# A two-layer graph network on one core: the opening stage reordered, the first group's weight factors read where they were made, x1 in four tiles

## The chip, the cores and the metric

The kernel runs on one core of a Trainium2 chip. The metric is the device time of that core in microseconds (us), from the start of the program to its end. All data are 32-bit floats.

The core has five engines that each run their own list of instructions in order. TensorE (PE) multiplies matrices; loading its stationary operand is shown apart as PEld. VectorE (DVE), ScalarE (ACT) and GpSimd (POOL) work element by element. SyncE (SP) issues transfers here. Engines wait for each other through semaphores, and an instruction that waits holds up all that stands behind it on its engine. Transfers between the large memory and the on-chip memory are served by 16 DMA engines.

## The reference

There are 128 batches of 128 nodes with 512 features, and one adjacency matrix `adj` of 128 x 128. Layer 0 normalizes each node, takes the positive part, mixes the nodes by `adj` and multiplies by a 512 x 512 weight; layer 1 is masked attention with 8 heads of 64, a projection, and a second normalization:

```python
h = jnp.maximum(_layernorm(x, axis=-1), 0.0)
x = x + (jnp.einsum('nm,bmd->bnd', adj, h) @ L0_weight + L0_bias)
h = jnp.maximum(_layernorm(x, axis=-1), 0.0)
q, k, v = heads of (h @ w_qkv)
attn = softmax(where(adj == 0, -inf, q @ k.T * scale))
o = (attn @ v) @ w_proj + b_proj
x = x + o + layernorm(o) * gamma + beta
```

## The kernel before

**Stages.** A batch passes through these steps; the names are those of tiles and functions in the code. `load` brings x. `norm0` takes statistics of x on VectorE, an inverse root `rs` on GpSimd and `shift` on VectorE; ScalarE makes h0 from them (L262), and GpSimd adds the bias of layer 0 to x (L265). `mix` multiplies h0 by the turned adjacency matrix on TensorE (L274) and ScalarE copies the result to yT. Layer 0's product with w0 follows, and VectorE adds x to it, which gives x1. `norm1` makes h1 in the same way (L318); h1 is written to the large memory and read back in four pieces (`exchange`, L208 and L213), so that VectorE's 32 x 32 transposes can finish the turn of the matrix (`flip`, L334). `keep_x1` adds beta to x1 on GpSimd (L325) and stores it as x1d, to be read again at the end. Then come q, k and v, the scores, the softmax, attention, projection and the output (`finish`, `finish_out`, `finish_last`).

**Seven products instead of eight.** Large products run as 2 x 2 blocks with seven block products (the Strassen-Winograd scheme). This needs sums of blocks on both sides. On the activation side GpSimd makes four sums (`left_factors`, L222; the tiles are hsum, ysum and osum). On the weight side four differences are made once (`combine_qkv`, `combine_one`, L149, on VectorE). For q, k and v a group of four batches is multiplied at once: three kinds (the three calls of `qkv` with kind 0, 1 and 2), seven products each (L362), from one weight block for each product. The weight blocks don't all fit on the chip. So the three plain blocks are fetched from the weight itself, and the four differences are first written to the large memory (`SUMS`, tile wt, L150) and fetched from there, into one of five tiles wq (`fetch`, L156). The differences are made in tiles that later stages use for other things: sx, pT, s, e, o, oT, x1b and t.

**The opening.** The first eight batches (`AHEAD`) run before anything else is there to overlap with. Their layer 0 is one plain product of eight matmuls for each batch (`layer0_whole`, L458, result pd), without the scheme. Its two result banks d0 and d1 alternate between batches, so the product of a batch waits until VectorE has added the result of the batch two before (L648). x1 has three tiles: the sum of batch 5 takes the tile of batch 2, and so waits for batch 2's store x1d.

**Order.** The code has no loop over stages. Each step is put into a list with a due time (`put`), the list is worked off by due time, and that fixes the order of instructions on each engine. The due times do not delay anything on the chip: they only set the order. `mix_at`, `h0_at`, `START` and `when` give the due times that the change touches. All transfers but a few at the start stand in one list, that of SyncE.

**Banks of the seven products.** Products 0 and 2 (counted from 0), then 4 and 6, collect in one bank, 1 and 3 in another, 5 in a third. A result is read out between two products of its bank, by ScalarE (`start`, L366) after products 0, 1, 2 and 6, and by VectorE (`add`, L251) after 3, 4 and 5. So product 4 waits until ScalarE has copied the result of product 2.

Of the kernel before, what the change touches and what calls it, by code (L numbers as in the profile page):

```python
# [9 lines left out]
F32 = mybir.dt.float32  # L10
AF = mybir.ActivationFunctionType
ALU = mybir.AluOpType
AX = mybir.AxisListType

P = 128
# [5 lines left out]
def kernel(  # L21
# [30 lines left out]
    nc = tc.nc  # L52
    B, N, D = x.shape
# [3 lines left out]
    G = 4  # L57
    Q, R = 4, 32
    F = D // 2
# [4 lines left out]
    work = ctx.enter_context(tc.tile_pool(name="work", bufs=2))  # L64
    stat = ctx.enter_context(tc.tile_pool(name="stat", bufs=8))
    dram = ctx.enter_context(tc.tile_pool(name="dram", bufs=3, space=bass.MemoryType.DRAM))
    psum = ctx.enter_context(tc.tile_pool(name="psum", bufs=1, space=bass.MemoryType.PSUM))
# [3 lines left out]
    X, H0, YT, X1, X1D, H1, H1T, WQ, QKT, V, S, PT, OT, O, X1B, LEFT0, LEFT1, LEFT2 = ({} for _ in range(18))  # L71

    def load(i):
        X[i] = work.tile([P, D], F32, name="x", bufs=6)
        nc.sync.dma_start(out=X[i], in_=x[i])
# [7 lines left out]
    w0_sb = const.tile([P, 7, 2, F], F32)  # L83
    wp_sb = const.tile([P, 7, 2, F], F32)
    b0_b = const.tile([P, D], F32)
    bp_b = const.tile([P, D], F32)
    gamma_b = const.tile([P, D], F32)
    beta_b = const.tile([P, D], F32)

    def block(w, row, col):  # L90

        return w[row * F:(row + 1) * F, col:col + F].rearrange("(c p) o -> p c o", p=P)

    BLOCKS = (0, 4), (5, 3)

    def load_square(eng, w_sb, w):

        for row, places in enumerate(BLOCKS):
            for col, k in enumerate(places):
                eng.dma_start(out=w_sb[:, k], in_=block(w, row, col * F))  # L100

    def broadcast(eng, t, src):
        eng.dma_start(out=t, in_=src.partition_broadcast(P))
# [9 lines left out]

        combine(eng, w[:, 0], w[:, 4], w[:, 5], w[:, 3], w[:, 1], w[:, 2], w[:, 4], w[:, 6])

    load_square(nc.scalar, w0_sb, w0)
    for i in range(2, 4):
        load(i)
    broadcast(nc.scalar, b0_b, b0)

# [2 lines left out]
    def qkv_block(kind, row, col):  # L125
        return block(w_qkv, row, 2 * D + col * F if kind == 2 else col * D + kind * F)
# [3 lines left out]
    def load_qkv(kind, *names):  # L130

        pieces = []
        for name, bufs, shape in names:
            t = work.tile(shape, F32, name=name, bufs=bufs)
            t = t if len(shape) == 2 else t.rearrange("p a b -> p (a b)") if len(shape) == 3 else \
                t.rearrange("p a b c -> p (a b c)")
            pieces += [t[:, n:n + D].rearrange("p (c o) -> p c o", c=2) for n in range(0, t.shape[1], D)]
        for n in range(4):
            nc.sync.dma_start(out=pieces[n], in_=qkv_block(kind, n // 2, n % 2))
        return pieces  # L140

    def combine_qkv(eng, t, kind, pieces):
# [15 lines left out]
    ident = const.tile([P, P], F32)  # L158
# [4 lines left out]
    maskb = const.tile([P, P], F32)  # L163

    def turn_adj():
        pa = psum.tile([P, P], F32, tag="at", name="pa", bufs=4)
        nc.tensor.transpose(pa, adj_sb, ident)
        nc.scalar.copy(adjT, pa)

    def make_mask():  # L170


        edge = const.tile([P, P], F32)
        some = const.tile([P, 1], F32)
        nc.vector.tensor_scalar(edge, adj_sb, 0.0, None, op0=ALU.not_equal)
        nc.vector.tensor_reduce(some, edge, AX.X, ALU.max)
        nc.vector.reciprocal(some, some)
        nc.vector.tensor_scalar(some, some, 0.0, None, op0=ALU.mult)
        nc.vector.tensor_scalar(edge, edge, 1.0, MASKED, op0=ALU.subtract, op1=ALU.mult)
        nc.vector.tensor_scalar(maskb, edge, some, None, op0=ALU.add)  # L180
# [22 lines left out]
    def exchange(t, dst, src):  # L203


        w = src.shape[2]
        d = dram.tile([P, Q, w], F32, name=f"d{w}")
        nc.sync.dma_start(out=d, in_=src)  # L208
        put(t, exchange_back, dst, d)
# [87 lines left out]

    def layer0_whole(i, t):
        p = whole(YT, i, lambda row, col: w0_sb[:, BLOCKS[row][col]])
        X1[i] = work.tile([P, D], F32, name="x1", bufs=3)  # L300
        put(t + 3.6, nc.vector.tensor_tensor, X1[i], p, X.pop(i), ALU.add)

    def layer0(j):
        for b in (2 * j, 2 * j + 1):
            X1[b] = work.tile([P, D], F32, name="x1", bufs=3)
        return pair_chain(LEFT0.pop(j), w0_sb, (X1[2 * j], X1[2 * j + 1]), (X.pop(2 * j), X.pop(2 * j + 1)),
                          "d0", "d1")

# [7 lines left out]
    def norm1_out(i, t, arg):  # L316
        h1 = work.tile([P, Q, C, R], F32, name="h1")
        nc.scalar.activation(h1.rearrange("p q c r -> p c q r"), X1[i].rearrange("p (c q r) -> p c q r", c=C, q=Q),  # L318
                             AF.Relu, **arg)
        H1[i] = work.tile([P, Q, C * R], F32, name="h1x")  # L320
        exchange(t + 4.5, H1[i], h1.rearrange("p q c r -> p q (c r)"))
        put(t + 1.5, keep_x1, i)

    def keep_x1(i):
        nc.gpsimd.tensor_tensor(X1[i], X1[i], beta_b, op=ALU.add)  # L325
        X1D[i] = dram.tile([P, D], F32, name="x1d", bufs=20)
        nc.sync.dma_start(out=X1D[i], in_=X1.pop(i))

# [153 lines left out]
        put(t + 3, finish_last, i, n, X1B.pop(i))  # L482

    def finish_last(i, n, x1):
        nc.gpsimd.tensor_tensor(n, n, x1, op=ALU.add)
        nc.sync.dma_start(out=out[i], in_=n)

# [8 lines left out]
    BEGIN, LAST, AHEAD = -3, B - G, 8  # L496
    START = BEGIN * SHORT - 38.5
    later, count = [], [0]

    def put(t, f, *a):  # L500
        count[0] += 1
        heapq.heappush(later, (t, count[0], f, a))

    def when(i, us):
        return i * SLOT + us if i >= 0 else i * SHORT + us * SHORT / SLOT

    def mix_at(i):
        return START + i * STEP if i < AHEAD else when(i - 10, (11.6, 9.2)[i % 2])

    def h0_at(i):  # L510
        return mix_at(i) - 1.2 if i < AHEAD else when(i - 11 - i % 2, 13.2 if i % 2 else 12)

    def run(make, times):

# [18 lines left out]
    t, last = when(LATE, 0), ""  # L533
# [8 lines left out]
    def scores_at(i):  # L542
        return when(i - i % 2, 2 + i % 2) if i < LATE else AT["s"][i - LATE]
# [20 lines left out]
    GROUP = (3.9, 6.5, 9.05, 13.3, 16.75), (1.5, 4.1, 6.7, 11.0, 14.4)  # L564
    for i in range(B):
        if i >= 4:
            put(START - 3 + i if i < 6 else mix_at(i - 6) + 10 if i < AHEAD + 6 else when(i - 13, 0), load, i)
        put(mix_at(i), mix, i, mix_at(i))
        put(scores_at(i), scores, i, scores_at(i))
        put(flip_at(i), flip_probs, i)  # L570
        put(attend_at(i), attend, i, attend_at(i))

    for j in range(B // 2):
        a, b = 2 * j, 2 * j + 1
        i = a - 8
        if a < AHEAD:
            t = mix_at(a) - 5
            put(t, norm0, j, t)
            for n in (a, b):
                t = mix_at(n) + 5.2  # L580
                put(t, layer0_whole, n, t)
            t += 4.4
            flips = t + 11.7, t + 12.7
        else:
            t = when(i - 3, 5.2)
            put(t, norm0, j, t)
            t = when(i - 1, 12)
            put(t, pair_left, j, t, 2.5, YT, LEFT0, "ysum")
            run(lambda j=j: layer0(j), [when(i, p) for p in PAIR[0]])
            t = when(i, PAIR[0][6]) + 1.5  # L590
            flips = when(i + 2, 7.5), when(i + 2, 9)
        put(t, norm1, j, t)
        put(flips[0], flip, a)
        put(flips[1], flip, b)

        i = a + 5
        t = attend_at(b) + 2
        if b < LAST:
            put(t, pair_left, j, t, 3.4 if i < LATE else 1.5, OT, LEFT2, "osum")
            n = 7 * (a - LATE + 4) // 2  # L600
            times = [when(i, p) for p in PAIR[1]] if i < LATE else AT["p"][n:n + 7]
            run(lambda j=j: project(j), times)
            ends = [((a, b), when(i + 1, 1.2) if i < LATE else times[6] + 2.2)]
        else:
            ends = []
            for n in (a, b):
                t = AT["D"][n - LAST]
                put(t, project_whole, n, t)
                ends.append(((n,), t + 4.6))
        for batches, t in ends:  # L610
            for n in batches:
                put(t - 7 + 3 * (n % 2), reload, n)
            put(t, finish, batches, t)

    steps = []
    for g in range(B // G):
        i = g * G - 3
        t, gap = (START + 36.2, 1.4) if g == 0 else (when(i - 1, 13), 4) if i < LATE else (TAIL + 9.8, 2.2)
        put(t, group_left, g, t, gap)
        times = sorted(when(i + n, p) for n in range(G) for p in GROUP[(i + n) % 2] + ((13.1,) if n == 0 else ()))  # L620
        if i + G > LATE:
            n = sum(t < TAIL for t in times)
# [2 lines left out]
            run(lambda g=g, kind=kind: qkv(g, kind), times[7 * kind:7 * kind + 7])  # L625
        steps += [(t, g, n // 7, n % 7) for n, t in enumerate(times)]
    for n, (t, *a) in enumerate(steps):
        put(steps[n - 4][0] + 0.1 if n >= 4 else t - 10, fetch, *a)

    put(START - 6, turn_adj)  # L630
    put(when(-2, 2), make_mask)
# [4 lines left out]
        put(t - 12, lambda kind=kind, t=t, tiles=tiles: combine_qkv(nc.vector, t, kind, load_qkv(kind, *tiles)))  # L636
    put(when(-2, 9), combine_square, nc.gpsimd, w0_sb)
    put(START + 8, broadcast, nc.sync, beta_b, beta)
    put(when(0, 12), load_square, nc.sync, wp_sb, w_proj)
    put(when(1, 3), broadcast, nc.sync, bp_b, b_proj)  # L640
    put(when(1, 4), broadcast, nc.sync, gamma_b, gamma)
    put(when(2, 12), combine_square, nc.gpsimd, wp_sb)
# [3 lines left out]
    while later:  # L646
        t, _, f, a = heapq.heappop(later)
# [30 lines left out]
```

## Time and profile before

| what | before |
|---|---|
| time, median of three runs | 2381.83 us (2381.12 to 2382.42) |
| span of the profiled run | 2388.1 us |
| TensorE busy, with 14105 matmuls | 2335.9 us, 98% |
| VectorE, ScalarE, GpSimd busy | 67%, 44%, 70% |
| idle time of TensorE from 0 to 90 us | 18.9 us |
| idle time of TensorE from 2250 us to the end | 21.9 us |
| start of the first qkv product | 52.61 us |
| start of the second kind's, of the third kind's first product | 76.6 us, 90.45 us |

The profile has groups of instructions, each with a line of the code, an engine, and its operands as `out<-in`. The idle time of an engine stands in brackets, with what ended it: `DMA wq<-wt` means that the data had not landed. TensorE runs at one of two clock rates, and PEclk or the clock column is the share of the full rate that was granted. 32-bit matmuls show as two records each, so eight records are four matmuls. A record's length holds a tail in which the next has begun; the difference between two starts is the better price.

### The profile page before, as it was taken

The numbers are of one execution on the slowest core, as the hardware profiler recorded it, in microseconds if no ns is written. First come the engines' busy times: TensorE is split into PE (matmuls) and PEld (weight loads), VectorE is DVE, ScalarE is ACT, GpSimd is POOL, SyncE is SP. The second block draws the span as 40 slices with busy tenths as digits, with TensorE's granted clock in tenths as the row PEclk, the third lists the DMA queues.
The fourth block names the chain that finished last, engine by engine and source line by source line (L and its number), as shares of the span: only waits on it lengthen the run. The fifth ranks groups of instructions, "written<-read, shape, count | busy, mean of one in ns | idle before, by whom it ended". The sixth has DMA issues, their size and how long they took to land.

```text
span 2388.1 us, 42653 instructions
## 1 busy us (share of the span) xinstructions
PE 2335.9 (98%) x14105; PEld 2052.5 (86%) x14105; DVE 1604.7 (67%) x3225; ACT 1044.4 (44%) x3074; POOL 1674.3 (70%) x1592
## 2 busy tenths in 40 slices
PE   7999999999999999999999999999999999999996
PEld 6788888888888888888888888888888888888885
DVE  5566676676666766766766667667666667666665
ACT  2344444444444544444444445344444444444442
POOL 4467677767777776777677777767766777777566
PEclk9999999999999999999999999999999999999998
DMA  7776766766767666667677676677676676776664
GB/s 232 241 230 217 230 219 217 232 218 221 228 213 231 218 216 220 222 205 232 209 230 226 216 230 217 210 231 221 216 231 210 221 226 212 233 226 202 221 208 146
DMA packets 400059, 524.35 MB, mean 220 GB/s; under 512 B 40032, under 2 KB 250336, under 8 KB 399840
## 3 DMA queue, kind: packets, MB, share of 16 engines
q1 hardware_dynamic: 398464, 520.25, 68.5%
q8 instruction: 113, 1.85, 0.3%
q10 hardware_dynamic: 1376, 1.38, 0.2%
q14 instruction: 106, 0.87, 0.1%
HBM read 350.55 MB, written 170.92 MB: 218 GB/s over the span
## 4 chain that ended last, share of the span: by engine, by line
PE 84%; DMA 6%; DVE 4%; POOL 3%; SPq 2%; issue 2%; ACT 1%; POOLq 0%; DVEq 0%; ACTq 0%
PE pc L362 37%; PE pd L288 24%; PE pz L362 6%; PE ps L382 5%; PE po L440 5%; PE pmix L274 4%; PE pz L288 4%; DMA sx<-d 2%; SPq L213 1%; DVE pT L431 1%; DMA wq<-in_L_gnn_w_qkv_dram 1%; DMA h1x<-d 1%; POOL t L481 1%; DMA wq<-wt 1%; ACT e L416 1%
## 5 line engine op out<-in xcount | busy, mean ns | idle before, releaser
L195 POOL TENSOR_TENSOR rs<-ve,minus_half 128x2 f32<-128x2 f32 (+1 forms) x194 | 136.0, 701 | 614.7 <-DVE ve L193 520.6
L362 PE MATMUL pc<-hsum,wq 128*128 128x256 f32 x2048 | 485.1, 380 | 9.8 <-DMA wq<-wt 4.3
L416 ACT ACTIVATE e<-s,mx 128x128 f32<-128x128 f32 x992 | 384.6, 389 | 180.6 <-DVE mx L396 114.8
L362 PEld LDWEIGHTS pc<-hsum,wq 128*128 128x128 f32 x2048 | 389.4, 191 | 65.1 <-POOL hsum L222 4.9
L425 POOL TENSOR_TENSOR e<-e,sm 128x1024 f32<-128x1024 f32 x124 | 237.5, 1915 | 32.1 <-DVE sm L424 26.8
L288 PE MATMUL pd<-wp_sb,osum 128*128 128x256 f32 x992 | 254.4, 379 | 0.7 <-DVE o L294 0.7
L362 PE MATMUL pc<-h1T,wq 128*128 128x256 f32 x1024 | 246.2, 384 | 0.4 <-DMA wq<-in_L_gnn_w_qkv_dram 0.4
L288 PE MATMUL pd<-w_sb,ysum 128*128 128x256 f32 x960 | 246.4, 379 | 0.0
L362 PE MATMUL pc<-wq,hsum 128*128 128x256 f32 x1024 | 245.0, 382 | 0.0
L431 DVE STREAM_TRANSPOSE pT<-sx 128x1024 f32<-128x1024 f32 x124 | 153.4, 1237 | 128.8 <-DMA sx<-d 126.7
L648 ACT COPY oT<-po 128x512 f32<-128x512 f32 x128 | 74.9, 586 | 370.3 <-PE po L440 370.3
L362 PEld LDWEIGHTS pc<-h1T,wq 128*128 128x128 f32 x1024 | 193.2, 191 | 29.8 <-DMA wq<-in_L_gnn_w_qkv_dram 0.8
L362 PEld LDWEIGHTS pc<-wq,hsum 128*128 128x128 f32 x1024 | 192.0, 190 | 28.6
L288 PEld LDWEIGHTS pd<-wp_sb,osum 128*128 128x128 f32 x992 | 184.0, 190 | 23.8 <-POOL rs L195 1.1
L366 ACT COPY qkT<-pc 128x512 f32<-128x512 f32 x256 | 144.4, 575 | 124.5 <-PE pc L362 124.2
L288 PEld LDWEIGHTS pd<-w_sb,ysum 128*128 128x128 f32 x960 | 177.9, 190 | 21.7
L390 DVE TENSOR_TENSOR s<-ps,maskb 128x512 f32<-128x512 f32 x256 | 159.1, 683 | 55.6 <-PE ps L382 55.6
L480 ACT ACTIVATE t<-o,shift,rs 128x512 f32<-128x512 f32 x128 | 103.2, 807 | 203.0 <-DVE shift L199 193.8
L416 ACT ACTIVATION_READ_ACCUMULATOR e<-s,mx 128x1 f32 x992 | 185.7, 187 | 0.0
L475 POOL TENSOR_TENSOR x1b<-x1b,o 128x512 f32<-128x512 f32 x120 | 152.7, 1273 | 35.4 <-DMA x1b<-x1d 31.9
L190 DVE BATCH_NORM_STATS2 st<-x 128x6 f32<-128x512 f32 x256 | 172.1, 672 | 3.0 <-DMA x<-in_x_dram 2.9
L481 POOL TENSOR_TENSOR t<-t,gamma_b 128x512 f32<-128x512 f32 x128 | 163.1, 1274 | 10.7 <-ACT t L480 10.7
(104 smaller groups left out, 4704.2 us busy)
## 6 DMA issues: line engine op xcount, KB each, us to landing
wq<-wt SPq DMA_DIRECT2D x384, 256.0 KB, 3.8
wq<-in_L_gnn_w_qkv_dram SPq DMA_DIRECT2D x288, 256.0 KB, 3.6
d<-e SPq DMA_DIRECT2D x124, 512.0 KB, 2.9
sx<-d SPq DMA_DIRECT2D x496, 128.0 KB, 2.9
x<-in_x_dram SPq DMA_DIRECT2D x128, 256.0 KB, 4.3
d<-h SPq DMA_DIRECT2D x128, 256.0 KB, 2.9
x1d<-x SPq DMA_DIRECT2D x128, 256.0 KB, 3.1
h1x<-d SPq DMA_DIRECT2D x512, 64.0 KB, 2.3
```

The costliest lines, as they stand in the source:

```text
L190: nc.vector.bn_stats(st, src)
L195: nc.gpsimd.tensor_tensor(rs, ve, minus_half[:, :w], op=ALU.pow)
L288: nc.tensor.matmul(p[:, 0, :], lhsT=left[k][:, c, :], rhs=w_sb[:, k, c, :], start=first and c == 0, stop=last and c == 1, skip_group_check ...
L362: nc.tensor.matmul(p[:, half, :], lhsT=lhsT, rhs=rhs, start=first and half == 0 and c == 0, stop=last and c == 1, skip_group_check=True)
L366: nc.scalar.copy(results[n], p)
L382: nc.tensor.matmul(ps[e][:, c, :], lhsT=qk[r, c, j % 2, :], rhs=qk[r, C + c, j % 2, :], start=True, stop=True)
L390: nc.vector.tensor_tensor(s[:, e * C:(e + 1) * C, :], ps[e], m4, op=ALU.add)
L416: nc.scalar.activation(e[:, :, h, :], s[:, h, :].rearrange("p (q r) -> p q r", q=Q), AF.Exp, bias=shift[:, h:h + 1], scale=scale, accum_ou ...
L425: nc.gpsimd.tensor_tensor(e, e, sm.unsqueeze(1).unsqueeze(3).to_broadcast([P, Q, H, R]), op=ALU.mult)
L431: nc.vector.transpose(PT[i].rearrange("p h (q r) -> p q h r", q=Q), S.pop(i).rearrange("p q (h r) -> p q h r", h=H))
L475: put(t + 1 + 3 * n, lambda i=i: nc.gpsimd.tensor_tensor(X1B[i], X1B[i], O[i], op=ALU.add))
L481: put(t + 1.5, lambda: nc.gpsimd.tensor_tensor(n, n, gamma_b, op=ALU.mult))
```

## The change

The change works on the first 100 us and on what the opening leaves for later stages.

- `turn_adj` gets five matmuls of the identity with itself before the transpose of `adj`, and eight after it. Their result isn't used.
- Two of the four blocks of w0 and the bias of layer 0 are loaded by SyncE's queue instead of ScalarE's.
- h0 of the first batches but the very first, and `norm0` of all pairs but the first, come about 3.5 us earlier in the list.
- x1 has four tiles.
- For the first eight batches beta is no longer added to x1 before the store, which then follows the sum at once. It is added to the last result in `finish_last`.
- The first group's weight blocks are not fetched. `load_qkv` enters the pieces that it holds, plain blocks and differences, in `WQ`, and TensorE reads them there. The differences are still written out for the other groups.
- x of batches 8 to 13 is loaded later, and the flips of batches 4 to 7 have a later place in the list.

```diff
-    def load_square(eng, w_sb, w):
+    def load_square(w_sb, w, engs):
         for row, places in enumerate(BLOCKS):
             for col, k in enumerate(places):
-                eng.dma_start(out=w_sb[:, k], in_=block(w, row, col * F))
+                engs[row].dma_start(out=w_sb[:, k], in_=block(w, row, col * F))
...
-    load_square(nc.scalar, w0_sb, w0)
+    load_square(w0_sb, w0, (nc.scalar, nc.sync))
     for i in range(2, 4):
         load(i)
-    broadcast(nc.scalar, b0_b, b0)
+    broadcast(nc.sync, b0_b, b0)
...
         for n in range(4):
             nc.sync.dma_start(out=pieces[n], in_=qkv_block(kind, n // 2, n % 2))
+        for k, n in enumerate((0, 4, 5, 3, 6, 2, 7)):
+            WQ[0, kind, k] = pieces[n]
         return pieces
...
     def turn_adj():
+        def idle(n):
+            p = psum.tile([P, P], F32, tag="c0", name="pidle", bufs=1)
+            for _ in range(n):
+                nc.tensor.matmul(p, lhsT=ident, rhs=ident, start=True, stop=True)
+
+        idle(5)
         pa = psum.tile([P, P], F32, tag="at", name="pa", bufs=4)
         nc.tensor.transpose(pa, adj_sb, ident)
         nc.scalar.copy(adjT, pa)
+        idle(8)
...
-        X1[i] = work.tile([P, D], F32, name="x1", bufs=3)
+        X1[i] = work.tile([P, D], F32, name="x1", bufs=4)
...
-        put(t + 1.5, keep_x1, i)
+        put(t + (1.5 if i >= AHEAD else 0), keep_x1, i)
     def keep_x1(i):
-        nc.gpsimd.tensor_tensor(X1[i], X1[i], beta_b, op=ALU.add)
+        if i >= AHEAD:
+            nc.gpsimd.tensor_tensor(X1[i], X1[i], beta_b, op=ALU.add)
...
     def finish_last(i, n, x1):
+        if i < AHEAD:
+            nc.gpsimd.tensor_tensor(n, n, beta_b, op=ALU.add)
         nc.gpsimd.tensor_tensor(n, n, x1, op=ALU.add)
...
     def h0_at(i):
-        return mix_at(i) - 1.2 if i < AHEAD else when(i - 11 - i % 2, 13.2 if i % 2 else 12)
+        if i < AHEAD:
+            return mix_at(i) - (4.6 if i else 1.2)
+        return when(i - 11 - i % 2, 13.2 if i % 2 else 12)
...
-            put(START - 3 + i if i < 6 else mix_at(i - 6) + 10 if i < AHEAD + 6 else when(i - 13, 0), load, i)
+            put(START - 3 + i if i < 6 else mix_at(i - 6) + 10 if i < AHEAD else when(max(i - 13, (i - 16) / 2), 0), load, i)
...
-            t = mix_at(a) - 5
+            t = mix_at(a) - (8.5 if a else 5)
...
-            flips = t + 11.7, t + 12.7
+            flips = (t + 11.7, t + 12.7) if a < G else (t + 16, t + 17)
...
     for n, (t, *a) in enumerate(steps):
-        put(steps[n - 4][0] + 0.1 if n >= 4 else t - 10, fetch, *a)
+        if a[0]:
+            put(steps[n - 4][0] + 0.1, fetch, *a)
...
-    put(when(0, 12), load_square, nc.sync, wp_sb, w_proj)
+    put(when(0, 12), load_square, wp_sb, w_proj, (nc.sync, nc.sync))
```

More of the change, by code (lines that the diff above doesn't have):

```diff
@@ L304, in layer0 @@
         for b in (2 * j, 2 * j + 1):
-            X1[b] = work.tile([P, D], F32, name="x1", bufs=3)
+            X1[b] = work.tile([P, D], F32, name="x1", bufs=4)
         return pair_chain(LEFT0.pop(j), w0_sb, (X1[2 * j], X1[2 * j + 1]), (X.pop(2 * j), X.pop(2 * j + 1)),
```

## The prediction

> **What bounds the kernel now.** I read three views. The page first: which engine is full, and where.
>
> ```profile
> PE 2335.9 (98%) x14105; PEld 2052.5 (86%) x14105; DVE 1604.7 (67%) x3225; ACT 1044.4 (44%) x3074; POOL 1674.3 (70%) x1592
> PE   7999999999999999999999999999999999999996
> ```
>
> TensorE works 98% of the span, and the only thin slices are the first and the last. So time can be won by less TensorE work (the change removes none), or by closing holes at the two ends. Second, busy time by stage (length, PE, PEld, DVE, ACT, POOL, granted clock, DMA share, GB/s):
>
> ```profile
> 0.00:44.00 44.00, 35.14 (x175) 31.25 (x176) 24.01 (x48) 14.94 (x22) 19.94 (x23) 1.00 0.62 203
> 44.00:90.00 46.00, 35.96 (x144) 29.06 (x143) 26.26 (x53) 9.37 (x15) 23.44 (x19) 0.85 0.92 297
> 140.00:500.00 360.00, 359.86 (x2196) 317.77 (x2195) 249.89 (x502) 163.47 (x489) 254.35 (x244) 1.00 0.70 221
> 2250.00:2388.00 138.00, 116.07 (x748) 99.47 (x746) 77.94 (x148) 52.07 (x171) 93.42 (x82) 0.95 0.58 186
> ```
>
> The first 90 us hold 18.9 us of TensorE idle time, and in the second half of them the clock is down and the DMA engines are 92% full. From 140 us on TensorE is idle 0.14 us in 360: whatever the head saves is carried to the end, unless the middle gets a new wait. The tail has 21.9 us of idle, but TensorE's order there is the same in both programs. Third, TensorE's timeline of the head (start, length; in brackets the idle time before and what ended it):
>
> ```profile
> 7.92 2.08 PE L274 MATMUL pmix<-adjT,h 128*128 128x128 f32 x8 [3.38 <-ACT h L262]
> 11.38 2.08 PE L274 MATMUL pmix<-adjT,h 128*128 128x128 f32 x8 [1.39 <-ACT h L262]
> 13.25 5.35 PE L458 MATMUL pd<-w_sb,yT 128*128 128x256 f32 x16
> 18.44 1.05 PE L274 MATMUL pmix<-adjT,h 128*128 128x128 f32 x8
> 19.33 3.62 PE L458 MATMUL pd<-w_sb,yT 128*128 128x256 f32 x16
> ...
> 47.40 5.38 PE L458 MATMUL pd<-w_sb,yT 128*128 128x256 f32 x16 [2.72 <-DVE x L648]
> 52.61 1.89 PE L362 MATMUL pc<-h1T,wq 128*128 128x256 f32 x8
> 55.67 1.99 PE L362 MATMUL pc<-hsum,wq 128*128 128x256 f32 x8 [1.17 <-POOL hsum L222]
> 58.57 3.72 PE L362 MATMUL pc<-hsum,wq 128*128 128x256 f32 x16 [0.90 <-POOL hsum L222]
> 66.55 3.75 PE L362 MATMUL pc<-hsum,wq 128*128 128x256 f32 x8 [4.26 <-DMA wq<-wt]
> 71.29 3.70 PE L362 MATMUL pz<-h1T,wq 128*128 128x256 f32 x8 [0.99 <-DMA wq<-in_L_gnn_w_qkv_dram]
> ```
>
> The same eight records of L274 take 2.08 and then 1.05, those of L362 1.89 and then 3.75: half speed at the start and after long waits. Starts of neighbours give the price at full speed: a mix 0.89 us, a whole layer-0 product 3.46, one of the seven qkv products 1.73.
>
> **What the Trainium skill says.** "TensorE: Matmul & The Clock Gate", Part 1, "What's actually happening": the half-rate clock is the default, released after about 3.4 us of busy time and back after an idle window; windows of 3413 ns run free. The trace agrees: 3.4 us slow from 47.5, 10.2 us from 64.5, and 3.4 us at 897, after a hole of only 1.90. I take a hole filling over half a window as enough. "SBUF — State Buffer", "SBUF: two separate sides": a VectorE operation with two SBUF inputs and a GpSimd operation exclude each other. It agrees: the factor subtractions of L149 take 0.65 to 1.75 us, the long ones beside GpSimd. "DMA: Bandwidth & Descriptors", "Anatomy of one DMA", gives some 2.0 us fixed per transfer; here a 64 KB exchange lands in a median 2.3 us, and at 92% load 256 KB ones need over 5.
>
> **The change, leg by leg.** A leg ends where TensorE starts the next kind of work.
>
> *Leg 1, up to the first qkv product (52.61).* Eight mixes and eight layer-0 products need 8 x (0.89 + 3.46) = 34.8 us at full speed. From 7.92 that would end at 42.7; it ends at 52.61. The 9.9 lost: slow clock for mixes 0 and 1 (2.2) and product 0 (1.7), a wait for h0 (1.4), the 2.72 wait (2.9 from start to start), the slow product after it (1.7). The edits aim at each:
> - Five matmuls of the identity before the transpose of adj and eight after it. The row of the transpose gives 0.44 each when cold: about 2.2 us inside the 4.1 now spent waiting for adj, and 3.5 us from 4.5 to 8.0 inside the wait for h0. They end when h0 is due, cost 0 to 0.3, and the clock should be up when mix 0 starts.
> - h0 of batch 1 moves ahead of yT of batch 0 on ScalarE: the 1.39 wait goes. h0 of later batches is also earlier.
> - w0 half on SyncE's queue, and the bias too: ScalarE's queue issues three transfers, not six, so its table load no longer waits until 5.60. Its h0 waits for the statistics of x at 6.85 anyway: 0.1.
> - x1 in four tiles and no beta before the store: the sum of batch 5 waits no more for x1d of batch 2 (the wait and its slow product, 4.6 together). Four tiles let batch 5 take batch 1's, whose store is issued some 12 us earlier.
> So leg 1 ends at about 8.0 + 34.8 = 42.8, say 43.0: 9.6 saved.
>
> *Leg 2, the first seven products (52.61 to 76.6, of which 7 x 1.73 = 12.1 is work).* 7.3 of waits and about 3.7 of slow clock. The two DMA waits (4.26, 0.99) go: 21 fetches of 256 KB, 5.5 MB, are left out, because the products read the pieces that the subtractions already hold. What ends last then? After the flip of batch 3 (end 53.91) VectorE has two subtractions, a sum, statistics of x1 of batches 6 and 7 and of x of 8 and 9, two more subtractions; then shift (63.1), two h1 on ScalarE (63.3 to 64.8) and, queued behind them, the copy of product 2, which product 4 waits for. From the trace that chain is flip + 11.4, or flip + 9.9 without the 1.49 in which it waited for x1d. It was hidden behind the 66.55 of the fetch, and becomes the bound.
> When is the flip? x1 of batch 3 is ready at about 27 (32.8 before); its exchange is behind four loads of weights, two results and a subtraction that waits for VectorE. Moving the issues of the trace up and taking 0.68 us per queued 256 KB, as in landings at 92% load, I get its last landing at 42 and the flip at 43.0. Product 4 then starts at 52.9. Products 0 to 3 run from 43.0 with about 1.0 of waits on hsum (beta no longer stands between two hsum on GpSimd) and end near 50: a hole of 2.9, enough for 3.4 us at half speed, 1.7. Products 4 to 6: 52.9 + 5.2 + 1.7 + 0.3 = 60.1. Leg 2 is 17.1 instead of 24.0: 6.9 saved.
>
> *Leg 3, second kind, two mixes (76.6 to 90.45).* 7 x 1.73 + 2 x 0.89 = 13.9, already dense: 0. Its pieces are in SBUF by about 50, the oT ones too.
>
> *Then.* Flips of batches 4 to 7 ended 25 us ahead of their use; x of 10 to 13, now loaded later, land some 6 us ahead by the same shifting. The in-place pieces sit in tiles whose next users (softmax, attend, output) come after those products. That adds one kind of wait: the first load into sx on SyncE's queue, and GpSimd's scaling of e, now also wait for TensorE's products of the first kind. Behind that load stand the next fetches, which the second group waits for; but the load was issued at 107.84 and those products ended at 76.6, so it costs nothing. The 1.66 wait at 121 follows TensorE's own chain and stays. Eight beta additions of 1.27 us move to GpSimd's output stage: 10.2 us on an engine busy 254 of 360, hidden by its idle time. Tail: 0.
>
> Sum: 9.6 + 6.9 = 16.5, so 2381.8 - 16.5 = 2365.3; I say 2366, as one more small wait is likelier than one fewer. Unknowns: the number of slow windows (0 to 3, 1.7 each, so -1.7 to +3.4), the flip of batch 3 (-1 to +3, by DMA load), the start (+-0.5).
>
> **Rivals.**
> - *The exchange stays where it was.* The queue was 92% full, and each issue waits its turn behind VectorE's subtractions; taking out 5.5 MB need not bring batch 3 forward. For: issues in order, landings of 5 us. Against: before 52 us only three fetches had been issued. Then only leg 1 counts: 2381.8 - 9.6 = 2372.2.
> - *No hole before product 4.* If VectorE's chain shortens without beta on GpSimd beside it, the 2.9 and the slow window go too: 16.5 + 4.6 = 21.1, 2360.7. For: subtractions of 1.1 to 1.7 us that could be 0.65. Against: four operations gain at most 3 us, and hsum still runs beside them.
> - *Slower.* Later x loads or held tiles block a queue in the first stages and eat the 16.5, and GpSimd's 10.2 us shows, since it feeds TensorE: 2381.8 + 10.2 = 2392. For: 70% busy, in order. Against: TensorE waited for GpSimd only 3.7 us in qkv products, all in the first 130 us except the tail's 1.8.
>
> **How the numbers follow.** Forecast 0.62, exchange 0.15, no hole 0.15, no measurable change by partial loss 0.03, slower 0.05. The range reaches to both faster rivals: 2360.5 to 2373. Faster 0.92, same 0.03, slower 0.05.
>
> **What would show it.** Mix 0 at about 8 taking 1.05 for eight records; first qkv product near 43 with no wait for x1d; no DMA wait in the first 14 products; product 4 near 53 behind ScalarE; the third kind near 74 (90.45 before); 140 us on and the tail as before. Wrong if a hole opens between 90 and 140, or if the identity matmuls end well after h0.

## The result, and the profile after

The changed kernel takes 2371.93 us (median of four runs, 2366.59 to 2375.05), the kernel before 2382.12 us beside it: 10.2 us less and a ratio of 0.9955 (95% interval 0.9934 to 0.9977). A second measurement of both, the first experiment below, gives 0.9937 (0.9923 to 0.9951), 2370.62 against 2386.40 us, 15.8 us less. The forecast was 2366, in a range of 2360.5 to 2373, and a gain of 15.8 us.

One kernel differs from one execution to the next by some us: in the second measurement before lay between 2380.18 and 2389.90 us, the changed kernel between 2366.26 and 2372.80. So times below are read with their intervals, and single traces for the place of a wait, not for a total.

The page of the changed kernel, the same two lines as before:

```profile
PE 2332.1 (98%) x14131; PEld 2051.9 (86%) x14131; DVE 1615.9 (68%) x3225; ACT 1044.7 (44%) x3074; POOL 1672.0 (70%) x1592
PE   8999999999999999999999999999999999999997
```

TensorE has 26 records more, two for each of the 13 identity matmuls (the 14105 of the kernel before are records too), and is yet busy 3.8 us less: less of its work ran at half speed. Its idle time, span less busy time, fell from 52.2 to 40.7 us. Busy time by stage (length, PE, PEld, DVE, ACT, POOL, granted clock, DMA share, GB/s; the last stage is the tail of the shorter span):

```profile
0.00:44.00 44.00, 41.19 (x223) 36.97 (x224) 27.28 (x55) 16.54 (x24) 15.84 (x21) 1.00 0.70 232
44.00:90.00 46.00, 40.00 (x206) 34.35 (x205) 28.49 (x56) 14.94 (x35) 21.95 (x20) 0.96 0.54 180
140.00:500.00 360.00, 356.16 (x2174) 313.35 (x2173) 248.37 (x495) 159.90 (x477) 263.52 (x252) 1.00 0.70 220
2235.00:2373.00 138.00, 118.27 (x755) 101.62 (x753) 79.80 (x150) 53.17 (x173) 93.43 (x82) 0.94 0.58 188
```

The first two rows hold most of the gain: TensorE is busy 10.1 us more in the same 90 us, 5.1 of them with the identity matmuls, and in the second row the DMA engines are at 54% where they were at 92%. The third row is the surprise: from 140 to 500 us TensorE is idle 3.84 us, where it was idle 0.14. TensorE's timeline of the head (start, length; idle time before and its end in brackets), with the line numbers of the changed file:

```profile
7.84 2.05 PE L284 MATMUL pmix<-adjT,h 128*128 128x128 f32 x16 [0.88 <-ACT h L272]
9.72 3.67 PE L470 MATMUL pd<-w_sb,yT 128*128 128x256 f32 x16
...
36.43 7.07 PE L470 MATMUL pd<-w_sb,yT 128*128 128x256 f32 x32
43.34 1.89 PE L374 MATMUL pc<-h1T,sx 128*128 128x256 f32 x8
48.39 3.72 PE L374 MATMUL pc<-hsum,s 128*128 128x256 f32 x16 [3.16 <-POOL hsum L232]
51.95 1.89 PE L374 MATMUL pc<-hsum,pT 128*128 128x256 f32 x8
56.68 3.58 PE L374 MATMUL pc<-hsum,e 128*128 128x256 f32 x8 [2.85 <-ACT qkT L378]
60.05 2.01 PE L374 MATMUL pz<-h1T,pT 128*128 128x256 f32 x8
...
77.50 1.89 PE L374 MATMUL pc<-oT,h1T 128*128 128x256 f32 x8
```

Two mixes now take 2.05 us together where each took 2.08. The products of batches 6 and 7 run on without a wait (x32). The qkv products read sx, s, pT and e, and no DMA wait is left among them. The third kind starts at 77.50 instead of 90.45 us, 12.95 earlier. What is left in leg 2 is a wait for hsum before product 1 and one for ScalarE's copy before product 4.

### The profile page after: what moved, and what is told of

It reads as the page before. It is cut to its first block, busy times and chain, and to the rows that moved or that the text cites. A ratio compares the mean times of both kernels' runs of the same rounds, so it can differ in the third digit from the quotient of the medians.

```text
span 2372.8 us, 42591 instructions
## 1 busy us (share of the span) xinstructions
PE 2332.1 (98%) x14131; PEld 2051.9 (86%) x14131; DVE 1615.9 (68%) x3225; ACT 1044.7 (44%) x3074; POOL 1672.0 (70%) x1592
## 4 chain that ended last, share of the span: by engine, by line
PE 86%; DMA 5%; DVE 4%; POOL 2%; issue 1%; SPq 1%; ACT 1%; DVEq 0%; POOLq 0%; ACTq 0%
PE pc L374 37%; PE pd L298 24%; PE pz L374 6%; PE po L452 5%; PE ps L394 5%; PE pmix L284 4%; PE pz L298 4%; DMA sx<-d 2%; SPq L223 1%; PE pd L470 1%; DVE pT L443 1%; DMA wq<-in_L_gnn_w_qkv_dram 1%; DMA x1b<-x1d 1%; DMA wq<-wt 1%; DVE v L261 1%
## 5 line engine op out<-in xcount | busy, mean ns | idle before, releaser
L374 PE MATMUL pc<-hsum,wq 128*128 128x256 f32 x1984 | 468.5, 379 | 3.2 <-POOL osum L232 1.8
L374 PEld LDWEIGHTS pc<-hsum,wq 128*128 128x128 f32 x1984 | 376.5, 190 | 55.7 <-POOL osum L232 2.2
L374 PE MATMUL pc<-h1T,wq 128*128 128x256 f32 x992 | 237.6, 382 | 0.7 <-DMA wq<-in_L_gnn_w_qkv_dram 0.7
L665 ACT COPY oT<-po 128x512 f32<-128x512 f32 x128 | 74.9, 586 | 370.4 <-PE po L452 370.4
L374 PE MATMUL pc<-wq,hsum 128*128 128x256 f32 x992 | 237.4, 382 | 0.4 <-DMA wq<-wt 0.4
L374 PEld LDWEIGHTS pc<-h1T,wq 128*128 128x128 f32 x992 | 185.9, 190 | 28.8 <-DMA wq<-in_L_gnn_w_qkv_dram 1.1
L374 PEld LDWEIGHTS pc<-wq,hsum 128*128 128x128 f32 x992 | 185.9, 190 | 28.5 <-issue 0.8
```

The source lines that it names most:

```text
L374: nc.tensor.matmul(p[:, half, :], lhsT=lhsT, rhs=rhs, start=first and half == 0 and c == 0, stop=last and c == 1, skip_group_check=True)
```

## The experiments

The starts are those of the run's traced execution, in us. Each ratio is to the kernel before, run beside it, with its 95% interval; since before's own median moved between 2382 and 2389 us from one set of runs to another (the experiments ran on four chips), the ratio is the column to compare. A difference of 0.0010 in it is 2.4 us.

| run | median us | ratio | first product | product 1 | product 4 | third kind |
|---|---|---|---|---|---|---|
| before (the profile ahead of the change) | 2381.83 | 1 | 52.6 | 55.7 | 66.6 | 90.5 |
| changed kernel (the result above) | 2371.93 | 0.9955 (0.9934-0.9977) | 43.3 | 48.4 | 56.7 | 77.5 |
| changed kernel again | 2370.62 | 0.9937 (0.9923-0.9951) | 43.7 | 48.3 | 56.7 | 75.7 |
| no identity matmuls | 2375.08 | 0.9957 (0.9943-0.9970) | 44.3 | 48.8 | 57.1 | 76.2 |
| x1 in three tiles | 2370.93 | 0.9939 (0.9925-0.9954) | 42.7 | 47.5 | 55.8 | 74.9 |
| fetches kept | 2378.79 | 0.9973 (0.9963-0.9983) | 43.3 | 48.8 | 60.5 | 83.9 |
| x loads early | 2373.38 | 0.9945 (0.9931-0.9959) | 42.7 | 48.6 | 56.8 | 76.0 |
| before, in place alone | 2382.07 | 0.9975 (0.9966-0.9984) | 48.6 | 52.8 | 62.1 | 82.9 |
| beta left out for eight batches | 2368.33 | 0.9923 (0.9909-0.9936) | 42.8 | 47.8 | 56.1 | 75.2 |
| beta early | 2368.91 | 0.9924 (0.9911-0.9938) | 42.8 | 47.4 | 55.7 | 76.5 |
| beta early, no identity matmuls | 2371.42 | 0.9934 (0.9918-0.9949) | 43.9 | 47.9 | 56.2 | 75.3 |
| head moves alone | 2375.00 | 0.9943 (0.9926-0.9961) | 43.0 | 44.7 | 51.6 | 77.4 |
| beta early and head moves | 2367.07 | 0.9916 (0.9903-0.9930) | 43.1 | 44.8 | 52.9 | 73.7 |
| the same, fourth sum first | 2364.74 | 0.9894 (0.9877-0.9910) | 42.8 | 44.5 | 49.7 | 73.5 |

**The changed kernel again.** No edit.

> The changed kernel once more, to see how far one execution differs from the next. Theory: the head is fixed (first qkv product near 43.3 us, third kind near 77.5 us), and what differs is the number of waits and slow clock windows in the middle; the median lies within 2368 to 2374. Rival: the head itself moves by some us from run to run with the phase of the clock's windows.

The first qkv product started at 43.7 us and the third kind at 75.7, against 43.3 and 77.5 in the first trace. The median lies where the theory had it, but the head is not fixed: it varies by 1 to 2 us, with the place of the slow clock, 6.8 us from 47.7 in this run and 3.4 us from 56.9 in the other. Product 4 starts at 56.7 us in both. In this run the slow clock stretches products 1 and 2 and fills the time in which TensorE would wait for product 4 anyway; in the other it comes behind product 4 and delays all that follows.

**No identity matmuls.**

```
-        idle(5)
...
-        idle(8)
```

> Without the 13 identity matmuls; nothing else changes. Theory: mixes 0 and 1 and product 0 run at half speed again (2.2 + 1.7 us), every later batch and the exchange of batch 3 move by the same, so the time rises by 3 to 4 us. Rival (the exchange is bound by the transfer queue, not by when it is fed): the delay is swallowed by the 3.2 us wait of qkv product 1, and the time rises by 0 to 1 us.

In the trace the rival holds: the first product is 0.6 to 1.0 us later than in the changed kernel's two traces, product 1 is 0.4 us later, and the third kind (76.2) lies between the two. TensorE's timeline of this run:

```profile
7.84 3.62 PE L282 MATMUL pmix<-adjT,h 128*128 128x128 f32 x16 [3.19 <-ACT h L270]
11.30 3.62 PE L468 MATMUL pd<-w_sb,yT 128*128 128x256 f32 x16
```

The two mixes take 3.62 instead of 2.05 us, but product 0 is at full speed already. With h0 of batch 1 moved ahead, TensorE works without a break from 7.84 on, and the clock came up at 11.2 us. But the time rose by 4.5 us by medians, a little more than the theory's 3 to 4, though the intervals still overlap. The trace shows waits of 2.82 and 1.90 us at 233 and 311 us, with 6.8 and 3.4 us of slow clock after them; whether these belong to the edit, one trace can't tell, and the run with beta early below was made for it.

**x1 in three tiles.**

```
-        X1[i] = work.tile([P, D], F32, name="x1", bufs=4)
+        X1[i] = work.tile([P, D], F32, name="x1", bufs=3)
```

> x1 in three tiles again, all else as changed. The prediction's step: the sum of batch 5 waits for the store of batch 2, the wait and a slow product cost 4.6 us. Rival, from the trace of the changed kernel: the store of batch 2 lands at 38.6 us, the sum of batch 5 would be at 35.8, so layer 0 ends 2.8 us later, but qkv product 1 waits until 48.4 us for the exchange of batch 3 anyway; the time rises by 0 to 1 us.

No change. The sum does wait for the store again, as VectorE's timeline of this run shows:

```profile
38.16 0.69 DVE L665 TENSOR_TENSOR x<-pd,x 128x512 f32<-128x512 f32 x1 [3.17 <-DMA x1d<-x]
```

But it still ends before the product of batch 7 is due at 39.3, and TensorE does not wait. Batch 2's store landed at 38.0 us here and at 46.4 before. With three tiles that is enough, so it is not the fourth tile that removed the 2.72 us wait but the earlier landing of this store. The store is no longer held for GpSimd's beta, the queue ahead of it is lighter, and the opening itself runs some 5 us earlier. No run separates the three; the lighter queue alone, in the kernel before (below), left 1.59 us of the wait.

**Fetches kept.** The entries into `WQ` and the condition `if a[0]` are taken back, so the first group's 21 blocks are fetched.

> The first group's 21 weight blocks are fetched again as before, all else as changed. Theory: the fetches stand in the queue among the exchanges and the differences, product 4 waits for its fetch, not for ScalarE, and the time rises by 5 to 8 us. Rival (what ends last is the chain over VectorE and ScalarE, so that the fetches were nearly hidden): it rises by 0 to 2 us.

The time rises by 8.2 us, just above the theory's 5 to 8, and the third kind starts 6.4 to 8.2 us later. TensorE's timeline names it:

```profile
60.52 3.75 PE L372 MATMUL pc<-hsum,wq 128*128 128x256 f32 x8 [4.57 <-DMA wq<-wt]
64.07 3.17 PE L372 MATMUL pz<-h1T,wq 128*128 128x256 f32 x8
```

The fetch of a difference holds product 4, 3.8 us later than ScalarE's copy does in the changed kernel, and slow clock follows. The theory holds.

**Before, in place alone.** The same two edits of `WQ` and `fetch`, in the kernel before.

> The kernel before with one edit: the first group's weight blocks are read where they were made, not fetched. Theory: the two waits for fetches go (5.3 us in the trace of before), but the chain over VectorE and ScalarE after the flip of batch 3 ends only 1.2 us earlier, so with the lighter queue the third kind starts 2 to 4 us earlier and the time falls by 2 to 4 us. Rival (the fetches were what bound leg 2): it falls by 6 to 8 us.

Ratio 0.9975, 5.8 us by medians, and the third kind 7.5 us earlier than in the trace of before: more than the theory's 2 to 4, a little less than the rival's 6 to 8. The reason is in leg 1, which I had not counted: the lighter queue lets batch 2's store land at 44.1 instead of 46.4 us, and the first qkv product starts at 48.6 instead of 52.6 us. The other 3.5 us of the third kind are as the theory has them. After that product 4 waits 2.59 us for ScalarE's copy, as forecast for the whole change. The two parts of the change work on the same queue, so their gains don't add: the fetches are worth 5.8 us taken out alone and 8.2 us put back last.

**x loads early.**

```
-            put(START - 3 + i if i < 6 else mix_at(i - 6) + 10 if i < AHEAD else when(max(i - 13, (i - 16) / 2), 0), load, i)
+            put(START - 3 + i if i < 6 else mix_at(i - 6) + 10 if i < AHEAD + 6 else when(i - 13, 0), load, i)
```

> The changed kernel with x of batches 8 to 13 loaded at the places of before. Theory: two to three loads of 256 KB stand ahead of the exchange of batch 3 on the transfer queue, 0.7 us each, so its flip and what follows are 1.5 to 2 us later, and the time rises by 1 to 2 us. Rival (they fill gaps of the queue): no change beyond 0.7 us.

The time is 2.8 us higher by medians (intervals overlapping), but not for the reason given: the last piece of batch 3's exchange landed at 45.84 us against 45.65 in the changed kernel, and the third kind starts at 76.0. The trace's waits are elsewhere, 2.08 us at 231 and five of 0.5 to 0.9 from 271 to 454 us. Those at 231, 271 and 307 us stand where the changed kernel waits too, for the reason that the next experiment finds; why they are longer with the loads early stays open.

**Beta left out, and beta early.** The first run leaves the addition out, for the first eight batches. The second moves it:

```
     def finish_last(i, n, x1):
-        if i < AHEAD:
-            nc.gpsimd.tensor_tensor(n, n, beta_b, op=ALU.add)
...
-                put(t - 7 + 3 * (n % 2), reload, n)
+                put(t - (7 if n >= AHEAD else 12) + 3 * (n % 2), reload, n)
+                if n < AHEAD:
+                    put(t - 0.5, lambda n=n: nc.gpsimd.tensor_tensor(X1B[n], X1B[n], beta_b, op=ALU.add))
```

> The changed kernel without the addition of beta to the first eight batches, which leaves that part of the computation out. Theory: the two additions before an output's store hold that store back, the reads of the softmax exchange stand behind the store on SyncE's queue, VectorE waits for them in its transpose, and TensorE waits for VectorE; without them the waits near 160, 233, 271 and 308 us (2.4 to 4.9 us in all, and slow clock after the longer ones) are gone, and the time falls by 3 to 6 us. Rival (the waits come from the phase that the shorter head leaves): they stay, and the time moves by less than 1.5 us.

> The changed kernel with the full computation, but beta is added for the first eight batches to the reloaded x1, ahead of the inverse roots of the output stage, where GpSimd waits 2.7 us for VectorE; the reload is issued 5 us earlier in the list. Theory: as without the additions, the waits near 160, 233, 271 and 308 us go and the time falls by 3 to 6 us against the changed kernel. Rival (it is the added work of GpSimd, not its place, that shows): the waits stay or move, and the time moves by less than 1.5 us.

Of the waits named, those near 233, 271 and 308 us go. The one near 160 us does not: it comes ahead of the first addition of beta, at 187.2 us, and is 1.19 us long with beta left out. TensorE's waits from 140 to 330 us, in total, times, and the longest: the changed kernel,

```profile
PE pd L298 <- DVE x L261: 3.4, 4, 1.2
PE pc L374 <- DMA wq<-wt: 0.4, 1, 0.4
```

with beta left out,

```profile
PE pd L298 <- DVE x L261: 1.6, 2, 1.2
PE pc L374 <- DMA wq<-wt: 0.4, 1, 0.4
```

and with beta early:

```profile
PE pc L374 <- ACT e L428: 0.9, 1, 0.9
PE pd L298 <- DVE x L261: 0.3, 1, 0.3
```

At the three places the changed kernel waits 3.2 us in each of its two traces, the run without beta 0.4 us and the run with beta early 0.3 us. The traces of all runs in the table sort the same way. With beta added in `finish_last` (seven traces) TensorE is idle for 3.1 to 6.0 us between 140 and 500 us, with beta elsewhere or left out (seven traces, the kernel before among them) for 0.1 to 2.2 us. The phase that a shorter head leaves is not what makes these waits: the two runs here have the changed kernel's head. Nor is it the amount of GpSimd's work, which with beta early is busy 265.9 us of the same stretch, against 263.5 us in the changed kernel.

The two runs lie within 0.6 us of each other. They are 2.3 and 1.7 us below the changed kernel by medians of different sets, and 3.3 and 3.1 us by the ratios, the low end of the 3 to 6 I expected; the intervals of the ratios (0.9909-0.9936, 0.9911-0.9938) overlap that of the changed kernel (0.9923-0.9951), so the times alone do not prove it. The mechanism is shown by the traces. In the changed kernel, around 230 us, on GpSimd:

```profile
223.93 1.28 POOL L498 TENSOR_TENSOR t<-t,beta_b 128x512 f32<-128x512 f32 x1
225.29 1.27 POOL L499 TENSOR_TENSOR t<-t,x1b 128x512 f32<-128x512 f32 x1
```

and behind it on SyncE's queue:

```profile
226.59 0.34 SPq L500 DMA_DIRECT2D out_dram<-t  x1
227.02 1.82 SPq L223 DMA_DIRECT2D sx<-d  x4
```

VectorE's timeline there:

```profile
231.44 1.25 DVE L443 STREAM_TRANSPOSE pT<-sx 128x1024 f32<-128x1024 f32 x1 [3.73 <-DMA sx<-d]
```

TensorE's timeline there:

```profile
233.65 1.13 PE L298 MATMUL pd<-w_sb,yT 128*128 128x256 f32 x4 [1.23 <-DVE x L261]
```

Beta ends, the last sum ends at 226.56, and the output's store is issued at once. Behind it stand the four reads of the softmax exchange, which have nothing to do with this output. VectorE's transpose waits for them, VectorE's sum of a layer-0 result stands behind the transpose, and TensorE needs that sum's bank. The queue's own waits (total, times, longest) put a size on it, from 190 to 340 us in the kernel before and from 180 to 330 in the changed one. Before:

```profile
SPq L486 <- POOL t L485: 19.6, 8, 5.1
```

The changed kernel:

```profile
SPq L500 <- POOL t L499: 30.0, 8, 6.7
```

10.4 us more over eight stores, and eight additions of 1.27 us are 10.2. With beta early it is 20.3 us, with beta left out 19.1 us.

**Beta early, no identity matmuls.** Both edits from above.

> Beta early, and no identity matmuls: the first trial without them rose by 4.4 us, though its trace showed the third kind no later (76.2 us) and two waits of 2.8 and 1.9 us in the stages with beta. Theory: those waits made the rise; with beta early the time rises by 0 to 1.5 us, since the half-speed start is swallowed by the wait of qkv product 1. Rival: the slow start does cost 3 to 4 us, and the third kind starts that much later.

The third kind starts at 75.3 us, 1.2 earlier than with the matmuls, so the rival's late start is not there. The time is 2.5 us higher by medians, more than the theory's 0 to 1.5 (ratio 0.9934 against 0.9924, intervals overlapping). Both trials without the matmuls came out slower, by 4.5 and 2.5 us, and neither trace shows it before the third kind. In this trace TensorE is idle for 6.3 us between 1000 and 2000 us, where beta early has 2.1, and nothing ties those waits to the edit. So the reason I gave for the matmuls is not shown, and what they are worth stays open between 0 and some 4 us.

**The moves of the head.** Three changes of order, with the aim of a version better than both:

```
-        nc.sync.dma_start(out=d, in_=t)
+        if d is SUMS[0, 1] or d is SUMS[0, 2] or d is SUMS[0, 4] or d is SUMS[0, 6]:
+            put(START + 33, nc.sync.dma_start, d, t)
+        else:
+            nc.sync.dma_start(out=d, in_=t)
...
+        if g == 0 and kind == 0:
+            after[2] = 0.5
...
-            flips = (t + 11.7, t + 12.7) if a < G else (t + 16, t + 17)
+            flips = (t + 11.7, t + 12.7) if a < G else (t + 17.2, t + 18)
...
-        put(t - 12, lambda kind=kind, t=t, tiles=tiles: combine_qkv(nc.vector, t, kind, load_qkv(kind, *tiles)))
+        put(t - (5.5 if kind == 1 else 12), lambda kind=kind, t=t, tiles=tiles: combine_qkv(nc.vector, t, kind, load_qkv(kind, *tiles)))
```

The first edit puts the writes of the first kind's differences behind batch 3's exchange; the second shortens one interval in the list of products from 1.9 to 0.5, so that ScalarE's copy of product 2 comes earlier. The third puts the flips of batches 4 to 7 later, the last the second kind's loads and differences.

> The changed kernel with three moves in the order of its head: the exchanges of batches 2 and 3 ahead of the loads of the second kind's weight blocks and of the writes of the first kind's differences; ScalarE's copy of qkv product 2 ahead of h1 of batches 6 and 7; the flips of batches 4 and 5 after the sums of the first kind. Theory (two things end last in leg 2: the exchange of batch 3, then the chain over VectorE and ScalarE): the flip of batch 3 comes near 42 instead of 46.6 us, product 4 follows product 3 without a hole, the third kind starts near 70 us instead of 75.7 to 77.5, and the time falls by 5 to 8 us against the changed kernel. Rival (the transfer queue as a whole ends last, so that what is put first only delays what comes next): the third kind still starts after 75 us and the time moves by less than 2 us.

Of the theory only the first step came true. The flip of batch 3 ended at 43.1 us, product 1 started 3.6 to 3.7 us earlier, and product 12 started at 66.4 instead of 71.4 to 73.2 us, but product 4 still waited, 1.49 us for a sum of GpSimd. Then a longer wait came further on, in TensorE's timeline of this run:

```profile
66.37 1.89 PE L377 MATMUL pz<-h1T,s 128*128 128x256 f32 x8
...
72.13 3.78 PE L377 MATMUL pc<-h1T,o 128*128 128x256 f32 x8 [3.87 <-DVE qkT L264]
75.70 1.91 PE L287 MATMUL pmix<-adjT,h 128*128 128x128 f32 x8
```

VectorE's sum of the second kind stood behind the flips of batches 6 and 7, whose exchange is late on the queue; the hole brought 6.8 us of slow clock, and the third kind started at 77.4. The time did not fall (ratio 0.9943 against 0.9937, 1.4 us more), so the rival's numbers hold, and its reason as far as these two flips show it.

**Beta early and head moves.** With the flips of batches 6 and 7 also put later, `(t + 22.5, t + 23)`.

> Beta early, as in the run before, and the three moves of the head, with the flips of batches 6 and 7 also put after the sums of the second kind: in the run with the moves alone TensorE waited 3.9 us at product 13 for a sum that stood behind these two flips, whose exchange landed at 66 to 70 us. Theory: products 0 to 13 run with one hole of some 1.5 us, the third kind starts near 69 to 71 us, and the time is 2362 to 2366, 3 to 7 us below the run with beta early alone. Rival (what is put off on the transfer queue comes due in the third kind): the third kind starts early, but TensorE waits as much between 75 and 140 us, and the time stays at 2367 to 2370.

The third kind starts at 73.7 us, the time is 1.8 us below beta early (ratio 0.9916 against 0.9924, overlapping). The theory's start and time are not reached. The time is the rival's, but not for its reason: from 90 to 140 us TensorE is idle for 1.7 us, with beta early alone for 2.0. Product 4 waited 2.74 us, now for GpSimd's fourth sum, which stood behind an inverse root that waited 3.48 us for VectorE.

**The same, fourth sum first.** The sums are put at intervals of 1.1 in the list, not 1.4, which places the fourth ahead of that root.

> The kernel with beta early and the moves of the head, and one more move: GpSimd's fourth sum of the first group stands ahead of the inverse root of x1 of batches 6 and 7. In the trace of the run without this move the root waited 3.5 us for VectorE with the sum behind it, and product 4 waited 2.7 us for the sum and was followed by 3.4 us of slow clock. Theory: product 4 follows product 3; product 6 then waits 1 to 2 us for VectorE's sum; the third kind starts near 71 to 72 us instead of 73.7, and the time falls by 1.5 to 3 us, to 2364 to 2366. Rival (the wait only moves from product 4 to product 6): the third kind starts no earlier than 73 us and the time moves by less than 1 us.

TensorE's timeline of this run:

```profile
49.68 1.89 PE L377 MATMUL pc<-hsum,e 128*128 128x256 f32 x8
51.41 1.89 PE L377 MATMUL pz<-h1T,pT 128*128 128x256 f32 x8
56.16 3.45 PE L377 MATMUL pc<-h1T,e 128*128 128x256 f32 x8 [2.86 <-DVE qkT L264]
```

In the trace the rival holds: the hole moved from product 4 to product 6, and the third kind starts at 73.5. The median, 2364.74 us, lies where the theory had it. The ratio is 0.9894 (0.9877 to 0.9910), the lowest of all, and its interval lies wholly below the changed kernel's 0.9923 to 0.9951: this version, with the whole computation, is faster than both kernels. How much of its step from 0.9916 is this last move is not settled: the two intervals overlap, and the traced execution, which shows no earlier third kind, was the slowest of four (2368.95 us).

## Why the prediction was right, and where its terms were off

The direction, the place and the order of size were right: 2371.93 us in a range of 2360.5 to 2373, near its slow end, with most of the gain ahead of 90 us. The gain was forecast at 15.8 us and measured at 10.2 and then 15.8. That the second measurement meets the number is in part luck. In the traces the third kind starts 13.0 and 14.7 us earlier than before, and beta takes some 3 us back; the rest comes from waits and slow clock further on, which the prediction left out and which differ from trace to trace (idle time of TensorE from 500 to 2235 us: 9.1 us before, 6.4 and 4.3 us in the two traces of the changed kernel). By the steps:

- *Leg 1, end at 43.0.* Measured 43.3, and 42.7 to 43.7 over the runs with all its edits. The sum is right, its parts are not. The 4.6 us put down to x1 are not the fourth tile's: three tiles give the same time. The term belongs to the earlier landing of batch 2's store. And the 3.9 us of slow clock (2.2 and 1.7) put down to the identity matmuls do not return without them: the first product is then 0.6 to 1.0 us later.
- *Leg 2, 17.1 us.* Measured 20.3 us in the first trace (43.3 to 63.6) and 18.2 in the second. The mechanism is as forecast in the first trace: no fetch is waited for, a hole of 2.85 us before product 4 is ended by ScalarE's copy, and a slow window of 3.4 us follows. The chain from the flip of batch 3 to product 4 is 10.0 us (9.9 forecast). The mis-sized term is the flip: forecast 43.0, measured 46.6. VectorE's timeline of the changed kernel has the flips of batches 2 and 3:

```profile
44.74 0.71 DVE L346 STREAM_TRANSPOSE h1T<-h1x 128x512 f32<-128x512 f32 x1 [4.36 <-DMA h1x<-d]
45.95 0.69 DVE L346 STREAM_TRANSPOSE h1T<-h1x 128x512 f32<-128x512 f32 x1
```

Batch 3's last piece landed at 45.65, not 42. I had shifted the issues of the trace too far: h1 was ready at 33.6 us, but on SyncE's queue differences, results and a load stood between it and its read-back, and the eight pieces of batches 2 and 3 took from 38.43 to 44.09 to issue. The late flip also made the waits for hsum 3.16 us, where the prediction had 1.0. That the hole before product 4 has the forecast size (2.9) is luck: 43.0 + 4 x 1.73 + 1.0 is 50.9 and not "near 50", so the prediction's own terms leave a hole of 2.0, and in the trace both of its ends came later. In the second trace there is no hole there, since slow clock filled it. The list of leg 2's losses before (12.1 + 7.3 + 3.7) is 0.9 short of its 24.0, since the idle time before a product is less than the delay of its start; nothing rests on it.

- *Leg 3, 13.9 us.* 63.62 to 77.50 is 13.88.
- *"Hidden by its idle time": beta in the output stage, 0.* This step failed. GpSimd's load was the wrong measure. What counted was who stands behind the output's store on SyncE's queue, and the prediction had listed that question for sx alone. Idle time of TensorE between 140 and 500 us rose from 0.14 to 3.84 us; with beta early it was 2.2. In time it is worth 2 us by medians and 3 by ratios, near the 3.2 us of waits that go. With it the sign "140 us on ... as before" failed. It is close to the third rival, at a small part of its size and by another way: through the queue, not because GpSimd feeds TensorE.
- *The wait at 121.* It stayed, at 108.3 us: 1.21 us, and 1.67 in the second trace.

The exchange rival, 2372.2, is nearest in number, but its reason does not hold: batch 3's exchange did move, by 7.4 us (53.08 to 45.65), and the third kind by 12.95, more than leg 1's 9.6. The result lies there because leg 2 gave 3.7 to 5.8 us, not 6.9, and beta took some back. The second rival's reason came true in part: three subtractions that took 1.13 to 1.75 us take 0.64 to 0.67. But its hole remained in the first trace.

## What to carry to other kernels

Work moved to an engine that has idle time is free only if nothing urgent stands behind its result: follow the result to the queue that waits for it, and read what that queue carries next. Where one queue issues all transfers, a store that waits for a slow engine holds up reads that have nothing to do with it. And when the last of several waits is taken away, size the next one by the chain that stays, and expect one more behind it: the hole of this head stood ahead of products 1 and 4 in the changed kernel, then ahead of product 13, of 4 again and of 6, and of the three versions that moved it only the last is clear of the changed kernel in measured time.

## What the runs showed of the hardware

The clock fell after holes that were well below 3.4 us: after 1.90 us at 311 us of the run without identity matmuls and 2.08 us at 231 us of the run with early loads, but not after one of 3.16 us at 48 us of the changed kernel's first trace. The fourteen traces together show the rule. In each of them all recorded changes of the clock lie whole multiples of 3.413 us apart, so a trace can be cut into fixed windows of that length. Up to 2260 us, every full-speed window in which TensorE, by its timeline, was idle for 1.90 us or more is followed by half speed (21 windows, the least of them 1.90), and none with less is: in 59 of them the idle time was 1.0 to 1.77 us, and the clock stayed up. The hole of 3.16 us is cut by an edge into 1.40 and 1.76 us. A half-speed window was followed by full speed where TensorE was idle in it for 0.08 us or less (21 windows), and by half speed again where it was idle for 0.65 us or more (8 windows). So a whole idle window is not needed for the clock to fall, and the prediction's half a window (1.71 us) was close.

A window at half speed costs 1.7 us, half its length, where TensorE is what the stage waits for, and nothing where it fills a wait, as ahead of product 4 in the changed kernel's second trace. It is one part of what makes executions of one program differ, and not the whole: from 40 to 2260 us that trace has 6.8 us of slow clock and the first has 3.4, yet its span is 4.3 us shorter.
